# Two graph layers on one core: a changed order of evictions, GpSimd sums, row additions and norm steps within pairs of attention slots

## The chip, the cores and the metric

The kernel runs on one core of one Trainium2 chip. The metric is the device time of one execution in microseconds; a lower time is better. In texts and traces the engines are PE (TensorE, matmul), PEld (its weight loads), DVE (VectorE), ACT (ScalarE), POOL (GpSimd) and SP (SyncE, which issues most DMAs).

## What is computed

The input is `x` (8 graphs, 2048 nodes, 256 features) and one adjacency matrix (2048 x 2048). Two layers follow each other, each with a residual and a layer norm around it:

```python
# layer 0: attention, softmax inside chunks of 256 nodes, summed over the 8 chunks
scores = clip(einsum('bhnd,bhjcd->bhnjc', q, kc) / sqrt(64), -10, 10)
scores = where(mask == 0, -10.0, scores)
attn = softmax(scores, axis=-1)
ctx = einsum('bhnjc,bhjcd->bhnd', attn, vc)
out = ctx @ Wo.T + bo + x
out = layernorm(out) * gamma + beta          # norm "a"
x = layernorm(x + out)                       # norm "b"
# layer 1: graph attention
e = leaky_relu(s_src[:, :, None, :] + s_dst[:, None, :, :], 0.2)
alpha = softmax(where(mask, e, -inf), axis=2)
h_out = elu(einsum('bijh,bjhd->bihd', alpha, Wh))
x = layernorm(x + h_out)                     # norm "c"
```

## The kernel before, in words

All instructions are placed by hand: every engine works through its own list in the order in which the code emits it, and a tile framework adds the semaphores. So the order of the Python statements is the order on each engine.

**Batches and pairs.** The kernel runs over 8 batches (graphs). Layer 0 of a batch is 64 slots: four quarters `q` of 512 query nodes, two head pairs `hp`, eight chunks `c`. Two slots `s0`, `s1` make a pair, so a batch has 32 pairs `p`; within a quarter the pair has the step number `i`, 0 to 7. In batch `b`, layer 1 of batch `b - 1` runs along (`lower`, `along`): four tiles per pair, each made on VectorE by `make` (`e`, L779, three buffers) and multiplied on TensorE by `use` (`pa`, L801). `make` runs two tiles ahead of `use`, so the last pair of a batch finds only two tiles still to make. Batch 0 has no layer 1 beside it, and spends its first pairs on the mask steps (`Masks.step`) instead. Batch 7 leaves the last 18 slots (nine pairs) without it, since these tiles are kept for the stretch that follows. After the last batch, layer 1 of batch 7 runs alone.

**One pair.** In the iteration of pair `p`, `burst(p + 1)` computes the scores of the next pair: four blocks `ps` (L392), each in a pair of PSUM banks. The pairs of banks rotate among three tags (`two_banks`), and the blocks of a pair's two products (`product`, `pc`, L438) take part in that rotation, in the order ps, ps, ps, ps, pc, pc. An output block `po` (L585) or value block `pw` (L627), where a step has one, takes a turn too. VectorE evicts a score block with clip and mask (`evict`, `pr`, L404, from PSUM and one SBUF row tile), ScalarE takes the exponential (`exps`, L427). `product(s)` multiplies with the values on TensorE, and ScalarE copies the result (`raw`, L445). `normalize(s)` takes the reciprocal on VectorE (`rd`, L455) and then does two two-input rows on GpSimd: `part` (L462) and the addition to `acc` (L464).

The statements of the loop stand in this order before: normalize of the last slot; four score blocks with evictions 0 and 1; exp 0 and 1; make; eviction 2, exp 2; use, make, use, make; product s0; eviction 3, exp 3; normalize s0; use, make, use; the late hooks; product s1.

**Between the layers.** When a quarter's context is complete it goes out to DRAM and comes back transposed (`send_context`, `load_context`, `turn_context`). `Between` then does the rest of layer 0 in the pairs of the next quarter, and part of it in the quarter after that: bias, output projection, `y` (L596), norm "a" (`sums`, `squares`, `factors`, `apply`), the factor gamma (`scale`), the residual (`again`, L605), norm "b", the store of `x1D` (`finish`, L610), its transposed load and `turn`, and the value blocks of layer 1 (`values`). Tables (`FIRST_PAIRS`, `ON_ACT`, `LATE_ON`, `LAST_ON_PE`, `NEXT_...`) say at which step `i` and at which of several places in the pair each of these is emitted. The additions of the rows `bo`, `beta` and gamma (L569, L573, L602) run on GpSimd there, and the norm's mean and factors too. The tile `y` has one buffer. `Closing` does the end of layer 1 (residual `h`, norm "c", output) of batch `b - 2` in the first pairs of batch `b`, with its addition on GpSimd.

**Between batches.** After pair 31 a hand-written list `order` mixes the projections of the next batch (`project`: load, turn, keys, values, queries) with the last quarter's `Between` (`steps`, with row additions and statistics on VectorE) and the rest of the one before it (`early`).

Of the kernel before, what the change touches and what calls it, by code (L numbers as in the profile page):

```python
# [8 lines left out]
F32 = mybir.dt.float32  # L9
# [5 lines left out]
ALU = mybir.AluOpType  # L15
# [7 lines left out]
def adj_resnorm_kernel(  # L23
# [37 lines left out]
    assert D == 64 and KC == HP and 2 * D == P and sum(BANKS) == NT  # L61

    SQ = 32
    QS = HP * NK
# [17 lines left out]
    big = ctx.enter_context(tc.tile_pool(name="big", bufs=1))  # L82
    prp = ctx.enter_context(tc.tile_pool(name="prp", bufs=7))
    ep = ctx.enter_context(tc.tile_pool(name="ep", bufs=3))
# [409 lines left out]
    class Norm:  # L494
# [22 lines left out]

        def sums(self, ks):
            for k in ks:
                junk = small.tile([P, F], BF16, tag="junk", name="junk", bufs=1)  # L520
                nc.scalar.activation(
                    junk, self.src[:, k, :], AF.Copy, accum_out=self.mv[:, k, 0:1]
                )

        def centre(self):
            self.mean = small.tile([P, QT], F32, tag="mean", name="mean_" + self.name)
            nc.gpsimd.tensor_scalar(self.mean, self.mv[:, :, 0], -1.0 / F, None, ALU.mult)

        def squares(self, ks):
            for k in ks:  # L530
                junk = small.tile([P, F], BF16, tag="junk", name="junk", bufs=1)
                nc.scalar.activation(
                    junk,
                    self.src[:, k, :],
                    AF.Square,
                    bias=self.mean[:, k : k + 1],
                    accum_out=self.mv[:, k, 1:2],
                )

        def factors(self):  # L540
            self.rs = small.tile([P, QT], F32, tag="rs", name="rs_" + self.name)
            self.off = small.tile([P, QT], F32, tag="off", name="off_" + self.name)
            nc.gpsimd.tensor_scalar(self.rs, self.mv[:, :, 1], 1.0 / F, EPS, ALU.mult, ALU.add)
            nc.gpsimd.tensor_tensor(self.rs, self.rs, nhalf, ALU.pow)
            nc.gpsimd.tensor_mul(self.off, self.mean, self.rs)

# [11 lines left out]
    class Between:  # L558
# [3 lines left out]
        def __init__(self, b, g, sd, waug):  # L562
            self.b, self.g, self.sd, self.waug = b, g, sd, waug
            self.r = load_x(b, g, "xg")
            self.y = blocks.tile([P, QT, F], F32, tag="y", name="y", bufs=1)

        def bias(self, by):
            row = bo_sb.unsqueeze(1).to_broadcast([P, QT, F])
            by.tensor_add(self.r, self.r, row)  # L569

        def shift(self, by):
            row = beta_sb.unsqueeze(1).to_broadcast([P, QT, F])
            by.tensor_add(self.r, self.r, row)  # L573

# [24 lines left out]

        def scale(self, by):  # L600
            row = gamma_sb.unsqueeze(1).to_broadcast([P, QT, F])
            by.tensor_mul(self.y, self.y, row)  # L602

# [39 lines left out]

    FIRST_PAIRS = {
        2: lambda o: o.add((0, 1)),
        3: lambda o: o.add((2, 3)),
    }
    ON_ACT = {
        2: lambda o: o.a.sums((0, 1)),
        3: lambda o: o.a.sums((2, 3)),  # L650
        4: lambda o: o.a.squares((0, 1, 2, 3)),
        5: lambda o: o.a.apply(o.y),
        7: lambda o: o.b2.sums((0, 1, 2, 3)),
    }
    LATE_ON = {
        1: lambda o: o.bias(nc.gpsimd),
        3: lambda o: (o.a.centre(), o.shift(nc.gpsimd)),
        4: lambda o: o.a.factors(),
        5: lambda o: o.scale(nc.gpsimd),
        6: lambda o: o.again(),  # L660
        7: lambda o: o.b2.centre(),
    }
    LAST_ON_PE = {
        1: lambda o: o.output((0, 1)),
        2: lambda o: o.output((2, 3)),
    }
    NEXT_FIRST = {2: lambda o: o.load()}
    NEXT_ON_ACT = {
        0: lambda o: o.b2.squares((0, 1, 2, 3)),
        1: lambda o: o.finish(),  # L670
    }
    NEXT_LATE = {
        0: lambda o: o.b2.factors(),
        3: lambda o: o.turn(),
    }
    NEXT_LAST = {
        4: lambda o: o.values((0, 1)),
        5: lambda o: o.values((2, 3)),
    }
# [176 lines left out]
    class Close:  # L856
# [8 lines left out]

        def add(self, by=nc.vector):
            by.tensor_add(self.h, self.h, self.x)
            self.n = Norm(self.h, "c")
# [43 lines left out]
    HOME = (blocks, "xb", 2)  # L912
    HOME_Y = (blocks, "y", 1)
    HOME_PR = (prp, "pr", 7)

    class Closing:
# [5 lines left out]
        def do(self, s, *kinds):  # L922
            for g, step, *more in self.table.get(s, ()):
                if step not in kinds:
                    continue
                if step == "load":
                    self.of[g] = Close(self.b, g, *more)
                elif step == "finish":
                    self.of[g].finish()
                elif step == "add":  # L930
                    self.of[g].add(*more)
                elif step == "stats":
                    self.of[g].n.stats((0, 1, 2, 3))
                elif step == "most":
                    self.of[g].add_most()
                elif step == "sums":
                    self.of[g].n.sums((0, 1, 2, 3))
                elif step == "centre":
                    self.of[g].n.centre()
                elif step == "squares":  # L940
                    self.of[g].n.squares((0, 1, 2, 3))
                elif step == "factors":
                    self.of[g].n.factors()
# [27 lines left out]

    def closing_of(first, loads):
        table = {}
        for g, (i, (at, home)) in enumerate(zip(first, loads)):
            table.setdefault(at, []).append((g, "load", home))
            table.setdefault(i, []).append((g, "add", nc.gpsimd))
            table.setdefault(i + 1, []).extend([(g, "sums"), (g, "centre")])
            table.setdefault(i + 2, []).extend([(g, "squares"), (g, "factors")])
            table.setdefault(i + 3, []).append((g, "finish"))
        return table  # L980

    CLOSING = closing_of((0, 1, 3, 5), ((-1, HOME), (0, HOME), (2, HOME_Y), (4, HOME)))
    CLOSING_ALONE = {
# [25 lines left out]
    for b in range(B):  # L1009
# [16 lines left out]
        for p in range(PAIRS):  # L1026
# [22 lines left out]
            if p == PAIRS - 2 and b + 1 < B:  # L1049
                turns = [project(b + 1, g) for g in range(NCH)]  # L1050
                turns[0].pop(0)()

            if p:
                normalize(s0 - 1)
            hook(FIRST_PAIRS, NEXT_FIRST)
            if more:
# [4 lines left out]
                exps(*us[1])  # L1061
            hook(ON_ACT, NEXT_ON_ACT)
            if closing:
                closing.do(p, "sums", "squares", "finish")

            if along:
                along.rest(1)
                along.make()
            if more:
                evict(*waiting[1][0], waiting[1][1])  # L1070
                exps(*us[2])
            if along:
                along.use()
                along.make()
                along.use()
                along.make()
            elif not lower and masks.left():
                masks.step()
            product(s0)
            if more:  # L1080
                evict(*waiting[2][0], waiting[2][1])
                exps(*us[3])
            normalize(s0)
            if along:
                along.rest(1)
                along.use()
                along.make()
                along.use()
            elif not lower and masks.left():
                masks.step()  # L1090
            if i == 0 and q:
                send_context(b, q - 1, 1)
            if i == QP // 2:
                send_context(b, q, 0)
            if i == 1 and q:
                turn_context(q - 1, 1)
            if i == QP // 2 + 2:
                turn_context(q, 0)
            hook(LATE_ON, NEXT_LATE)
            if closing:  # L1100
                closing.do(p, "add", "centre", "factors")
            if p == PAIRS - 1 and b + 1 < B:
                turns[0].pop(0)()
            product(s1)
            hook(LAST_ON_PE, NEXT_LAST)
        normalize(SLOTS - 1)
# [4 lines left out]
        group = None  # L1111
        every = tuple(range(QT))

# [9 lines left out]
        def start_next():  # L1123
# [3 lines left out]
        early = [  # L1127
            lambda: before.b2.squares(every),
            lambda: before.b2.factors(),
            lambda: before.finish(),  # L1130
# [6 lines left out]
        steps = [  # L1137
            lambda: group.bias(nc.vector),
            lambda: group.output(every, parts),
            lambda: group.add(every),  # L1140
            lambda: (group.shift(nc.vector), group.a.stats(every)),
            lambda: group.a.apply(group.y),
            lambda: (group.scale(nc.vector), group.again(), group.b2.stats(every)),
            lambda: group.finish(),
# [86 lines left out]
```

## Time and profile before

| What | Value |
|---|---|
| Median of 3 runs | 3864.47 us (3863.78 to 3865.68) |
| The profiled execution's own time | 3871.02 us |
| Its span, first to last instruction | 3869.2 us |
| Mean granted clock of TensorE | 0.985 |
| Loop of batch 0 (pairs 0 to 30) | 291.9 us |
| Loop of batch 1 | 379.0 us |
| Loops of batches 2 to 6 | 382.6 to 384.2 us |
| Loop of batch 7 | 360.6 us |
| From the last pair of a batch to the first scores of the next | 73.0 (batch 0), 79 to 85 us |
| From the last pair of batch 7 to the end | 291.3 us |

The page gives busy time by engine and groups of instructions by line: busy time, mean length of one, then the idle time of the engine ahead of them and who ended it. A line of waits reads: who waited, for whom, microseconds in total, number of times, the longest. A line of a stretch gives its bounds, its length, busy time and instructions of each engine, and then the granted clock, the DMA share and the DMA rate. A loop in the table is measured from the first score matmul of one pair to that of another.

### The profile page before, as it was taken

What the parts mean: (1) busy time and instruction counts of PE and PEld (TensorE: products, weight loads), DVE (VectorE), ACT (ScalarE), POOL (GpSimd) and SP (SyncE); (2) the same over time, 40 slices, a digit from 0 to 9 for tenths busy, and PEclk for the clock granted to TensorE, in tenths of its full rate; (3) what the DMA queues carried; (4) which work ended last, traced back from release to release, by engine and by line L of the source; (5) the groups of instructions that cost most, each with busy time, mean ns of one, the idle gap of its engine ahead of it and who ended that gap; (6) DMA issues with size and microseconds to landing.
All of it is one profiled execution on the core that took longest, in us unless ns stands there. A gap on an engine that the chain in (4) does not pass through costs nothing.

```text
span 3869.2 us, 168899 instructions
## 1 busy us (share of the span) xinstructions
PE 3608.6 (93%) x76884; PEld 2625.2 (68%) x76884; DVE 3037.3 (78%) x3397; ACT 2262.8 (58%) x4211; POOL 1868.2 (48%) x1442
## 2 busy tenths in 40 slices
PE   8999999999999899999999999999999999999787
PEld 5655676766767667676767767777676766776676
DVE  5875688867888488885988848887688866886799
ACT  4776456656656565664756557655566656666322
POOL 0555245545555365553655536555355545555300
PEclk9999999999999999999999999999999999999899
DMA  6743333334333343333433334333443334333354
GB/s 163 159 103 71 87 96 100 105 72 120 100 99 100 72 125 98 104 99 80 118 100 97 93 100 122 97 92 82 106 114 105 103 69 115 102 101 87 85 149 136
DMA packets 635262, 399.03 MB, mean 103 GB/s; under 512 B 423216, under 2 KB 521904, under 8 KB 634544
## 3 DMA queue, kind: packets, MB, share of 16 engines
q1 hardware_dynamic: 584544, 354.53, 36.0%
q10 hardware_dynamic: 50000, 33.70, 2.8%
q8 instruction: 601, 9.85, 1.1%
q14 instruction: 117, 0.96, 0.1%
HBM read 331.22 MB, written 56.89 MB: 100 GB/s over the span
## 4 chain that ended last, share of the span: by engine, by line
PE 53%; DVE 25%; issue 9%; POOL 4%; ACT 4%; DMA 3%; SPq 0%; DVEq 0%; ACTq 0%; POOLq 0%
PE pc L438 15%; PE ps L392 14%; PE pa L801 13%; DVE e L779 10%; DVE pr L404 9%; PE pp L337 4%; PE pw L627 3%; PE pv L353 2%; POOL part L462 2%; POOL xg L569 1%; DMA x1D<-y 1%; PE po L585 1%; ACT y L549 1%; ACT raw L445 1%; DVE y L605 1%
## 5 line engine op out<-in xcount | busy, mean ns | idle before, releaser
L427 ACT ACTIVATE pr<-pr 128x1024 f32<-128x1024 f32 x1024 | 1077.1, 1056 | 960.2 <-DVE pr L404 940.8
L779 DVE SCALAR_TENSOR_TENSOR e<-srow,gd,et 128x1024 f32<-128x1024 f32 x1024 | 1385.0, 1379 | 17.4 <-PE pa L801 13.7
L404 DVE SCALAR_TENSOR_TENSOR pr<-ps,slab 128x1024 f32<-128x1024 f32 x1024 | 1217.5, 1214 | 118.8 <-PE ps L392 90.8
L801 PEld LDWEIGHTS pa<-waug,e 128*64 128x64 f32 x32768 | 1026.4, 140 | 278.9 <-issue 168.3
L801 PE MATMUL pa<-waug,e 128*64 128x65 f32 x32768 | 1100.6, 225 | 80.8 <-DVE e L779 74.9
L462 POOL TENSOR_TENSOR part<-raw,rd 128x512 f32<-128x512 f32 x448 | 634.5, 1416 | 992.5 <-DVE rd L455 982.1
L438 PE MATMUL pc<-vaug,pr 128*64 128x65 f32 x32768 | 1048.4, 223 | 6.4 <-issue 6.0
L392 PE MATMUL ps<-qT,kT 64*64 64x512 f32 x8192 | 977.0, 601 | 74.3 <-DVE pr L404 34.6
L438 PEld LDWEIGHTS pc<-vaug,pr 128*64 128x64 f32 x32768 | 1003.3, 138 | 29.2 <-DVE pr L404 18.1
L464 POOL TENSOR_TENSOR acc<-acc,part 128x512 f32<-128x512 f32 x448 | 668.8, 1493 | 35.1
L392 PEld LDWEIGHTS ps<-qT,kT 64*64 64x64 f32 x8192 | 271.7, 132 | 605.2 <-issue 242.2
L445 ACT COPY raw<-pc 128x520 f32<-128x520 f32 x512 | 297.5, 582 | 66.1 <-PE pc L438 63.0
L455 DVE RECIPROCAL rd<-raw 128x8 f32<-128x8 f32 x512 | 100.7, 197 | 284.7 <-ACT raw L445 284.7
L462 POOL TENSOR_TENSOR acc<-raw,rd 128x512 f32<-128x512 f32 x64 | 117.3, 1833 | 386.3 <-DVE rd L455 386.3
L337 PE MATMUL pp<-xT,wk_sb 128*128 128x512 f32 x256 | 135.7, 680 | 35.3 <-DVE xT L299 31.6
L596 DVE TENSOR_TENSOR y<-po,xg 128x512 f32<-128x512 f32 (+1 forms) x56 | 43.0, 768 | 155.1 <-POOL xg L569 67.7
L833 ACT ACTIVATE sums<-sums,dn 128x64 f32<-128x64 f32 x504 | 131.9, 335 | 21.7 <-DVE dn L827 12.8
L585 PE MATMUL po<-wo_sb,qT 128*64 128x256 f32 (+1 forms) x912 | 124.9, 382 | 12.5 <-DVE qT L482 11.8
L627 PE MATMUL pw<-w_sb,x1T 128*64 128x264 f32 (+1 forms) x800 | 125.8, 392 | 4.0 <-DVE x1T L299 4.0
L337 PEld LDWEIGHTS pp<-xT,wk_sb 128*128 128x128 f32 x256 | 53.7, 218 | 103.8 <-issue 63.5
L353 PE MATMUL pv<-wv_sb,xT 128*128 128x256 f32 x512 | 115.9, 379 | 0.0
L337 PE MATMUL pp<-xT,wq_sb 128*128 128x512 f32 x256 | 115.9, 595 | 0.0
(129 smaller groups left out, 2198.9 us busy)
## 6 DMA issues: line engine op xcount, KB each, us to landing
et<-edgeD SPq DMA_DIRECT2D x512, 256.0 KB, 3.1
slab<-clipD SPq DMA_DIRECT2D x256, 256.0 KB, 3.5
srow<-rowD SPq DMA_DIRECT2D x64, 512.0 KB, 4.9
xg<-in_x_dram SPq DMA_DIRECT2D x32, 512.0 KB, 5.0
x1D<-y ACTq DMA_DIRECT2D x32, 512.0 KB, 4.4
x1g<-x1D SPq DMA_DIRECT2D x32, 512.0 KB, 5.1
out_dram<-x1g SPq DMA_DIRECT2D x30, 512.0 KB, 4.0
ctxD<-acc ACTq DMA_DIRECT2D x56, 256.0 KB, 4.0
```

Of the source, the lines that this page charges most:

```text
L337: nc.tensor.matmul(pps[c], lhsT=w[:, kc, c * P : (c + 1) * P], rhs=st["xT"][:, kc, :], start=(kc == 0), stop=(kc == KC - 1),)
L353: nc.tensor.matmul(pv[:, u, :], lhsT=st["xT"][:, kc, u * P : (u + 1) * P], rhs=wv_sb[:, kc, :], start=(kc == 0), stop=(kc == KC - 1),)
L392: nc.tensor.matmul(ps[z * D : (z + 1) * D, k, :], lhsT=kT[rows, hp, t * P + z * D : t * P + (z + 1) * D], rhs=qT[rows, hp, cols], start=Tr ...
L404: nc.vector.scalar_tensor_tensor(pr, ps, -CLIP, row.unsqueeze(1).to_broadcast([P, 2, CH]), op0=ALU.max, op1=ALU.min,)
L427: nc.scalar.activation(pr, pr, AF.Exp, scale=0.125)
L438: nc.tensor.matmul(pc[z * D : (z + 1) * D, k, to], lhsT=probs[s][u][:, k, i * P + z * D : i * P + (z + 1) * D], rhs=vaug[:, KT * c + u, 2 ...
L445: nc.scalar.copy(raws[s].rearrange("p k i d -> p k (i d)"), pc[:, :, : QT * D1])
L462: nc.gpsimd.tensor_mul(part, raw[:, :, :, :D], rd.to_broadcast([P, 2, QT, D]))
L464: nc.gpsimd.tensor_add(accv, accv, part)
L627: nc.tensor.matmul(pw[z, k, : F + 2 * H], lhsT=self.x1T[:, c, u * P + z.start : u * P + z.stop], rhs=w1_sb[:, c, :], start=(c == 0), stop= ...
L779: nc.vector.scalar_tensor_tensor(e[:, :w], self.rows[n][:, :w], self.gd[:, h, j : j + 1], self.edge[k // JG][:, j % JG, :w], op0=ALU.max, ...
L801: nc.tensor.matmul(self.pa[i // QT][z * D : (z + 1) * D, i % QT, :], lhsT=e[:, i * P + z * D : i * P + (z + 1) * D], rhs=self.waug[:, j, h ...
```

## The change

The order within a pair becomes: normalize of the last slot; four score blocks with evictions 0 and 1; exp 0 and 1; make, use, make; the middle hooks (row additions, turns); product s0; normalize s0; evictions 2 and 3; the hooks on ScalarE; exp 2; use, make, use, make, use; the end hook; product s1; exp 3. The number of tiles made and used per pair stays four. The additions of the rows and the closing addition move from GpSimd to VectorE. `y` gets two buffers and `pr` six instead of seven. Most norm steps move a pair later, `bias` stays at step 1 but goes to the middle of the pair, `again` moves from step 6 to the end of step 7. `sums` folds the factor of the mean into its scale, so `centre` goes, and `factors` does its two scalar rows on VectorE. In `closing`, the last two loads go to the `y` buffers, and the table is written out. After the loop, the statistics of `before.b2` are taken on VectorE (`stats`).

```diff
-    prp = ctx.enter_context(tc.tile_pool(name="prp", bufs=7))
+    prp = ctx.enter_context(tc.tile_pool(name="prp", bufs=6))
...
         def factors(self):
...
-            nc.gpsimd.tensor_scalar(self.rs, self.mv[:, :, 1], 1.0 / F, EPS, ALU.mult, ALU.add)
+            nc.vector.tensor_scalar(self.rs, self.mv[:, :, 1], EPS, None, ALU.add)
+            nc.vector.tensor_scalar(self.off, self.mv[:, :, 0], ROOT_F, None, ALU.mult)
             nc.gpsimd.tensor_tensor(self.rs, self.rs, nhalf, ALU.pow)
-            nc.gpsimd.tensor_mul(self.off, self.mean, self.rs)
+            nc.gpsimd.tensor_mul(self.off, self.off, self.rs)
...
-            self.y = blocks.tile([P, QT, F], F32, tag="y", name="y", bufs=1)
+            self.y = blocks.tile([P, QT, F], F32, tag="y", name="y")
...
-    FIRST_PAIRS = {
-        2: lambda o: o.add((0, 1)),
-        3: lambda o: o.add((2, 3)),
+    FIRST_OF = {
+        3: lambda o: o.add((0, 1)),
+        4: lambda o: o.add((2, 3)),
+    }
+    MIDDLE_OF = {
+        1: lambda o: o.bias(),
+        4: lambda o: o.shift(),
+        7: lambda o: o.scale(),
     }
     ON_ACT = {
-        2: lambda o: o.a.sums((0, 1)),
-        3: lambda o: o.a.sums((2, 3)),
-        4: lambda o: o.a.squares((0, 1, 2, 3)),
-        5: lambda o: o.a.apply(o.y),
-        7: lambda o: o.b2.sums((0, 1, 2, 3)),
+        3: lambda o: o.a.sums((0, 1)),
+        4: lambda o: o.a.sums((2, 3)),
+        5: lambda o: (o.a.squares(every), o.a.factors()),
+        6: lambda o: o.a.apply(o.y),
     }
-    LATE_ON = {
-        1: lambda o: o.bias(nc.gpsimd),
-        3: lambda o: (o.a.centre(), o.shift(nc.gpsimd)),
-        4: lambda o: o.a.factors(),
-        5: lambda o: o.scale(nc.gpsimd),
-        6: lambda o: o.again(),
-        7: lambda o: o.b2.centre(),
+    END_OF = {
+        7: lambda o: o.again(),
     }
-    LAST_ON_PE = {
-        1: lambda o: o.output((0, 1)),
-        2: lambda o: o.output((2, 3)),
+    LAST_OF = {
+        2: lambda o: o.output((0, 1)),
+        3: lambda o: o.output((2, 3)),
     }
-    NEXT_FIRST = {2: lambda o: o.load()}
+    NEXT_FIRST = {3: lambda o: o.load()}
+    NEXT_MIDDLE = {4: lambda o: o.turn()}
     NEXT_ON_ACT = {
-        0: lambda o: o.b2.squares((0, 1, 2, 3)),
-        1: lambda o: o.finish(),
+        0: lambda o: o.b2.sums(every),
+        1: lambda o: (o.b2.squares(every), o.b2.factors()),
+        2: lambda o: o.finish(),
     }
...
     NEXT_LAST = {
-        4: lambda o: o.values((0, 1)),
-        5: lambda o: o.values((2, 3)),
+        5: lambda o: o.values((0, 1)),
+        6: lambda o: o.values((2, 3)),
     }
...
+    CLOSING = {
+        -1: [(0, "load", HOME), (1, "load", HOME)],
+        0: [(0, "add")],
+        1: [(0, "sums"), (1, "add")],
+        2: [(0, "squares"), (1, "sums"), (2, "load", HOME_Y)],
+        3: [(0, "finish"), (1, "squares")],
+        4: [(1, "finish"), (2, "add"), (3, "load", HOME_Y)],
+        5: [(2, "sums")],
+        6: [(2, "squares"), (3, "add")],
+        7: [(2, "finish")],
+        8: [(3, "sums")],
+        9: [(3, "squares")],
+        10: [(3, "finish")],
+    }
```

The loop after the change, from the bursts to the end of a pair:

```python
hook(FIRST_OF, NEXT_FIRST)
if p:
    normalize(s0 - 1)
if more:
    us = units_of(p + 1)
    waiting = burst(p + 1)
    evict(*waiting[0][0], waiting[0][1])
    exps(*us[0])
    exps(*us[1])
if along:
    along.rest(1)
    along.make()
    along.use()
    along.make()
elif not lower and masks.left():
    masks.step()
hook(MIDDLE_OF, NEXT_MIDDLE)
if closing:
    closing.do(p, "add")
...
product(s0)
normalize(s0)
if more:
    for us_ps in waiting[1:]:
        evict(*us_ps[0], us_ps[1])
hook(ON_ACT, NEXT_ON_ACT)
if closing:
    closing.do(p, "sums", "squares", "finish")
...
if more:
    exps(*us[2])
if along:
    along.rest(1)
    along.use()
    along.make()
    along.use()
    along.make()
    along.use()
elif not lower and masks.left():
    masks.step()
hook(END_OF, {})
...
product(s1)
if more:
    exps(*us[3])
hook(LAST_OF, NEXT_LAST)
```

After the loop: `early` begins with `before.b2.stats(every)` in place of `squares` and `factors`.

## The prediction

> **What bounds the kernel now.** I read the page's busy shares first, then who waited for whom, then the stretches of the loop one pair at a time, then single rows of the timeline.
>
> ```profile
> PE 3608.6 (93%) x76884; PEld 2625.2 (68%) x76884; DVE 3037.3 (78%) x3397; ACT 2262.8 (58%) x4211; POOL 1868.2 (48%) x1442
> ```
>
> TensorE is the bound: it idles 261 us of 3869. The only time to win is what it waits, and the waits name VectorE:
>
> ```profile
> PE pa L801 <- DVE e L779: 74.9, 96, 4.0
> PE ps L392 <- DVE pr L404: 34.6, 65, 4.6
> PE ps L392 <- DVE y L596: 29.4, 23, 1.5
> DVE y L596 <- POOL xg L569: 67.7, 23, 3.5
> DVE y L596 <- DMA x1D<-y: 65.5, 8, 11.1
> ```
>
> VectorE stands at `y` (L596) 67.7 us for GpSimd's bias row and 65.5 us for the store of the single `y` buffer, and TensorE's next scores stand behind it. Stretches of single pairs (first scores to first scores; length, busy PE, PEld, DVE, ACT, POOL):
>
> ```profile
> 2050.61:2065.33 14.72, 13.41 (x307) 9.46 (x305) 10.88 (x12) 6.30 (x10) 7.22 (x6) 1.00 0.43 90
> 2065.33:2076.54 11.21, 11.21 (x291) 8.67 (x289) 10.75 (x11) 6.27 (x11) 4.61 (x4) 1.00 0.24 63
> 330.66:338.14 7.48, 7.48 (x163) 4.94 (x161) 5.71 (x7) 4.96 (x9) 3.02 (x4) 1.00 0.02 8
> 338.14:347.39 9.25, 9.25 (x180) 5.91 (x176) 6.07 (x7) 7.60 (x15) 7.47 (x7) 1.00 0.23 58
> 2257.90:2261.30 3.40, 3.40 (x5) 1.35 (x5) 0.00 (x0) 0.07 (x1) 0.00 (x0) 0.50 0.47 159
> ```
>
> A pair beside layer 1 takes TensorE 11.21 us at best, a pair without it 7.48; an output or value block adds 9.25 - 7.48 = 1.77. The first row is such a pair with a block, 14.72 instead of 12.98. The last row shows the clock at a half for 3.4 us after TensorE stood idle for 4.36 us.
>
> [...] an eviction (one input in PSUM) is never stretched, `e` (two SBUF inputs) is.
>
> ```profile
> L404 DVE SCALAR_TENSOR_TENSOR pr<-ps,slab x1024: 1166/1215/1226, 70.8 to 3583.5; 128x1024 f32<-128x1024 f32 x171
> L779 DVE SCALAR_TENSOR_TENSOR e<-srow,gd,et x1024: 1228/1274/3405, 435.4 to 3852.4; 128x1024 f32<-128x1024 f32 x171
> ```
>
> [...] The rows give 2.35 to 2.43 against 1.22 us. [...]
>
> **The chain inside a pair.** Timeline rows (start, length):
>
> ```profile
> 1506.40 1.95 PEld L438 LDWEIGHTS pc<-vaug,pr 128*64 128x64 f32 x64
> 1508.60 0.59 ACT L445 COPY raw<-pc 128x520 f32<-128x520 f32 x1 [0.72 <-PE pc L438]
> 1510.23 0.20 DVE L455 RECIPROCAL rd<-raw 128x8 f32<-128x8 f32 x1
> 1510.34 1.24 DVE L779 SCALAR_TENSOR_TENSOR e<-srow,gd,et 128x1024 f32<-128x1024 f32 x1
> 1510.57 1.91 POOL L462 TENSOR_TENSOR part<-raw,rd 128x512 f32<-128x512 f32 x1 [6.45 <-DVE rd L455]
> 1528.03 1.28 POOL L464 TENSOR_TENSOR acc<-acc,part 128x512 f32<-128x512 f32 x1
> 1528.11 2.28 DVE L779 SCALAR_TENSOR_TENSOR e<-srow,gd,et 128x1024 f32<-128x1024 f32 x1
> ```
>
> So: product start to its copy 2.20, copy 0.6, reciprocal at +2.85, next VectorE row 0.11 later, GpSimd 0.35 after the reciprocal. A GpSimd row that meets an `e` waits for its end (1.91 instead of 1.04), and an `e` that meets a GpSimd row waits too (2.28). From the starts of following rows, evictions come every 1.135, `e` every 1.195; an eviction frees its bank 1.27 after its start.
>
> **The change, part by part.** Put 0 at the first score matmul of a pair.
>
> *Pairs beside layer 1.* New PE order: scores to 3.59, one use to 4.53, product s0 to 6.39, three uses to 9.19, product s1 to 11.21: the same work. New VectorE order: evictions 0 and 1 from 1.16 to 3.5, two `e` to 6.1 (0.2 for GpSimd included), then a row addition; the reciprocal of s0 can come at 4.53 + 2.85 = 7.38. So 1.3 us are free there, and a row addition of 1.17 costs nothing. Then evictions 2 and 3 from 7.49, beside GpSimd's two sums, which end 0.35 + 1.13 + 1.28 = 2.76 after the reciprocal, so the next `e` loses 0.2; two `e` to 12.37, the reciprocal of s1, and eviction 0 of the next pair at 12.48. It must free its bank before the three other score blocks end: 12.48 + 1.27 = 13.75 against 11.21 + 2.69 = 13.90. **The slack is 0.15 us.** What exceeds 1.3 in the first half or 0.15 in the second delays TensorE:
> - `again` now stands after the last `e` of step 7: 1.0, twice a batch (the third falls into the last pair).
> - step 4 of quarters 2 and 3: tail 0.28 + shift 1.17 + turn 1.20, less 1.3 and 0.15: 1.05 with the GpSimd stretch absorbed, twice.
> - squares (2.5 us on ScalarE) now before the third exp and layer 1's tail (1.27): the copy of s1 comes 0.7 late, 0.27 lost, five times. `factors` on VectorE, 0.3, hides where `e` would have waited for GpSimd.
> - closing in batches 2 to 7: pair 2 squares and sums (1.1), pair 3 finish, then squares, with `factors` behind them on VectorE (2.0), pair 6 addition beside tail and turn (1.1), pair 9 0.3: 4.5.
>
> Sum: 10.0 a batch. Before: a batch's 31 stretches should be 7.2 + 30 x 11.21 + 10 x 1.77 = 361.2; batches 2 to 6 took 383.3, so 22.1 were lost, mostly at steps 1 and 2 where `y` waited for the bias. Both go: the bias is on VectorE a step before. Gain 5 x 12.1 = 60; batch 1 (no closing) 17.8 less 5.5 = 12; batch 7's first 23 pairs 10. **Together -83.**
>
> *Pairs without layer 1* (batch 0 and the last nine of batch 7). The three PSUM pairs rotate, so product s1 takes the bank that eviction 2 frees. That eviction used to stand before product s0; now it stands behind its reciprocal, with no uses to cover it: 3.59 + 2.85 + 0.11 + 1.27 = 7.82 instead of 5.46. The pair becomes 9.69 instead of 7.48; with mask steps (17 pairs, 8.43 before) 10.15. Summed over batch 0, against its measured 292 and crediting the waits for the bias that go: +34. The end of batch 7: +10. TensorE now idles 1.9 to 2.2 us in each of these some 40 pairs. Gaps of 1.5 to 2.0 in batch 0 left the clock alone, one of 2.41 halved it. If a pair in two lost 1.7 us it would be 32 us, if none nothing; I take **16**. Together **+60**.
>
> *Between batches.* `y` has two buffers, so L596 starts with its matmul, not 2.5 us later. In the last pair no `e` is left in the second half (the tiles are exhausted), `scale` and `again` are on VectorE, and the next batch's first projection comes 0.6 earlier; GpSimd's last sums end sooner, and v0 starts 1.7 earlier. The chain then runs through ScalarE's key copies before `apply`: 2.4 earlier at k2. Six batches: **-15**. Could be -36, if the half clock at k2 goes too, or +10, if the load of `xg`, which waits for the later `again`, comes late.
>
> *At nothing:* one `pr` buffer fewer, since evictions 2 and 3 now follow the product that frees it; the folded scales of `sums` and `squares`; `centre` gone (0.23 on GpSimd); closing loads moved on SP, whose edge loads run six tiles ahead; VectorE's 117 us of row additions, in the 1.3 us hole except where listed. DMAs keep their number. The store of `x1D` on ScalarE's queue, the load of `x1t` on SP's and its turn move one pair later together; that load waits for a landing of 4.4 us, and the edge loads behind it are six tiles (1.5 pairs) ahead. The send of `ctxD` comes sooner on ScalarE's queue, ahead of exp 2; the sums that it waits for end near 3.9, before ScalarE gets there. The layer-1 end has no edited step.
>
> Sum: -83 + 60 - 15 = **-38 us**. The profiled execution took 3871.0 (span 3869.2), 0.17% over the median of 3864.5; the difference is taken from the median: **3826**.
>
> **The rivals.**
> 1. *The chain closes late* (slower). The slack of 0.15 is worked out from rows of another order. If `e` behind two sums starts later, or GpSimd beside evictions is slower, each of 208 pairs beside layer 1 loses the excess. From 0.15 + 38/208 = 0.33 us it outweighs everything; at 0.45 the time is 3826 + 62 = 3888. For it: nothing in the trace shows two sums, two evictions and two `e` in a row. Against: evictions never stretched.
> 2. *The change gives back what it takes.* The clock halves at every second short pair (+16) and the load of `xg` is late (+25): 3867.
> 3. *All covers hold*: no half clock in the short pairs, -36 between: 3789.
> 4. *It isn't what it says*: the sums still meet `e`. Then the same chain as rival 1, below its point.
>
> **How the numbers follow.** About 0.2% (8 us) is what a measurement here can tell from no change. Forecast (3806 to 3848) 0.42; rival 3 0.12; rival 2 and what lies between 0.22, of it 0.10 faster and 0.12 the same; rival 1, with 4, 0.24. So faster 0.64, same 0.12, slower 0.24. Range 3787 to 3892, from rival 3 to rival 1. The forecast's own is 3806 to 3848.
>
> **What would show it.** Right: pairs beside layer 1 at 11.21 with few exceptions, `e` near 1.28 throughout, no wait of `y` for POOL or for the store; batch 0 longer by some 35 us with PE `pc` waiting for DVE `pr`; PEclk at a half in places there. Wrong: pairs of 11.4 or more everywhere, with PE `ps` waiting for `pr`; or batch 0 unchanged.

## The result, and the profile after

| What | Before | After |
|---|---|---|
| Median | 3865.07 us (3863.78 to 3865.89) | **3800.70 us** (3793.95 to 3802.55) |
| The profiled execution's own time | 3871.02 us | 3793.95 us |
| Loop of batch 0 | 291.9 us | 335.9 us |
| Loops of batches 1 to 6, sum | 2295.7 us | 2202.4 us |
| Loop of batch 7 | 360.6 us | 358.1 us |
| Between batches, after batch 0; after 1 to 6, mean | 73.0; 82.0 us | 75.8; 77.8 us |
| From the last pair of batch 7 to the end | 291.3 us | 290.0 us |

The ratio is 0.9831, 95% interval 0.9814 to 0.9848: 1.7% faster. The profiled execution of after is the fastest of its runs, and that of before lies above all of its timed ones, so the two profiles differ by 77 us where the medians differ by 64. The stretches below are sums of the profiled 77.

The page's first lines of after, busy time by engine and the shares of the chain of waits:

```profile
PE 3570.4 (94%) x76884; PEld 2632.2 (69%) x76884; DVE 3079.9 (81%) x3701; ACT 2237.4 (59%) x4083; POOL 1390.2 (37%) x1202
...
PE 78%; DVE 13%; issue 5%; ACT 3%; DMA 1%; POOL 0%; DVEq 0%; ACTq 0%; SPq 0%; POOLq 0%
```

TensorE idles 222 us instead of 261. In the chain, VectorE had 25% before and GpSimd 4%; now it is 13% and nothing. Who waited for whom (total us, times, longest):

```profile
PE pc L440 <- DVE pr L406: 79.8, 57, 2.1
...
DVE y L602 <- PE po L591: 72.4, 55, 4.4
...
PE pa L805 <- DVE e L783: 38.5, 28, 4.0
...
PE ps L394 <- DVE pr L406: 22.8, 32, 4.3
```

Both waits of `y` that the prediction named (67.7 us for GpSimd's bias, 65.5 us for the store) are gone; `y` waits for its own matmul only. `pa` waiting for `e` has halved from 74.9. The first line is new, and it is the price: product s1 waits for eviction 2. The groups of `e` and of GpSimd's two sums (busy us, mean ns):

```profile
L783 DVE SCALAR_TENSOR_TENSOR e<-srow,gd,et 128x1024 f32<-128x1024 f32 x1024 | 1304.1, 1311 | 20.5 <-PE pa L805 11.2
...
L464 POOL TENSOR_TENSOR part<-raw,rd 128x512 f32<-128x512 f32 x448 | 481.0, 1074 | 1408.0 <-DVE rd L457 1401.4
...
L466 POOL TENSOR_TENSOR acc<-acc,part 128x512 f32<-128x512 f32 x448 | 581.0, 1297 | 35.2
```

Before, these means of `e`, `part` and `acc` were 1379, 1416 and 1493 ns. Of 448 `part` rows, 193 took over 1.2 us before and 16 do now. Stretches of single pairs: a pair beside layer 1; the one after an `again`; one with an output block; a short pair of batch 0; one with a mask step; the 3.41 us before a half-clock period, and most of that period (length, then busy PE, PEld, DVE, ACT, POOL, clock, DMA share, GB/s):

```profile
1547.18:1558.39 11.21, 11.21 (x292) 8.67 (x289) 11.12 (x12) 5.86 (x8) 4.66 (x4) 1.00 0.26 75
1558.39:1570.59 12.20, 11.44 (x293) 8.58 (x289) 11.42 (x14) 8.07 (x18) 3.37 (x3) 1.00 0.45 131
1487.56:1500.56 13.00, 13.00 (x309) 9.56 (x305) 12.46 (x14) 9.25 (x13) 6.03 (x6) 1.00 0.41 112
286.04:295.81 9.77, 7.69 (x162) 5.01 (x161) 7.87 (x9) 4.68 (x8) 3.37 (x3) 1.00 0.09 29
229.36:239.52 10.16, 8.47 (x175) 5.58 (x171) 8.39 (x12) 6.60 (x9) 4.66 (x4) 1.00 0.60 125
254.40:257.81 3.41, 1.36 (x48) 1.22 (x42) 2.66 (x5) 2.58 (x7) 0.98 (x1) 1.00 0.62 98
257.90:261.30 3.40, 3.40 (x64) 3.40 (x64) 1.43 (x3) 1.87 (x5) 2.50 (x3) 0.51 0.27 69
```

The timeline of the first of these pairs, from the end of product s0, shows the new order at work (start, length):

```profile
1554.52 0.20 DVE L457 RECIPROCAL rd<-raw 128x8 f32<-128x8 f32 x1
...
1554.64 2.31 DVE L406 SCALAR_TENSOR_TENSOR pr<-ps,slab 128x1024 f32<-128x1024 f32 x2
1554.87 1.04 POOL L464 TENSOR_TENSOR part<-raw,rd 128x512 f32<-128x512 f32 x1 [3.85 <-DVE rd L457]
...
1555.99 1.29 POOL L466 TENSOR_TENSOR acc<-acc,part 128x512 f32<-128x512 f32 x1
...
1556.86 2.69 DVE L783 SCALAR_TENSOR_TENSOR e<-srow,gd,et 128x1024 f32<-128x1024 f32 x2
...
1559.48 1.21 DVE L611 TENSOR_TENSOR y<-y,xg 128x1024 f32<-128x1024 f32 x1
...
1560.62 0.19 DVE L457 RECIPROCAL rd<-raw 128x8 f32<-128x8 f32 x1
...
1560.73 2.30 DVE L406 SCALAR_TENSOR_TENSOR pr<-ps,slab 128x1024 f32<-128x1024 f32 x2
```

The two sums run beside two evictions without loss (1.04 and 1.29 us, the evictions 2.31) and end 2.76 us after the reciprocal, as predicted; the two `e` lose 0.26 (2.69 instead of 2.43, which the two from 1563.54 on take). `again` (L611) sits ahead of the second reciprocal, and the next pair takes 12.20 instead of 11.21. A short pair of batch 0 in the same view:

```profile
289.63 2.09 PE L440 MATMUL pc<-vaug,pr 128*64 128x65 f32 x64
291.82 0.59 ACT L447 COPY raw<-pc 128x520 f32<-128x520 f32 x1 [1.18 <-PE pc L440]
...
292.44 0.20 DVE L457 RECIPROCAL rd<-raw 128x8 f32<-128x8 f32 x1 [0.61 <-ACT raw L447]
292.56 2.31 DVE L406 SCALAR_TENSOR_TENSOR pr<-ps,slab 128x1024 f32<-128x1024 f32 x2
293.80 2.09 PE L440 MATMUL pc<-vaug,pr 128*64 128x65 f32 x64 [2.08 <-DVE pr L406]
```

Product s0, its copy, the reciprocal, eviction 2 and product s1 follow each other in one string, with TensorE idle for 2.08 us in it.

### The profile page after: what moved, and what is told of

It reads as the page before. It is cut to its first block, busy times and chain, and to the rows that moved or that the text cites. A ratio compares the mean times of both kernels' runs of the same rounds, so it can differ in the third digit from the quotient of the medians.

```text
span 3792.1 us, 168780 instructions
## 1 busy us (share of the span) xinstructions
PE 3570.4 (94%) x76884; PEld 2632.2 (69%) x76884; DVE 3079.9 (81%) x3701; ACT 2237.4 (59%) x4083; POOL 1390.2 (37%) x1202
## 4 chain that ended last, share of the span: by engine, by line
PE 78%; DVE 13%; issue 5%; ACT 3%; DMA 1%; POOL 0%; DVEq 0%; ACTq 0%; SPq 0%; POOLq 0%
PE pc L440 23%; PE ps L394 21%; PE pa L805 19%; PE pp L339 6%; DVE pr L406 4%; DVE e L783 4%; PE pw L633 3%; PE po L591 3%; PE pv L355 2%; ACT raw L447 1%; ACT junk L536 1%; DVE y L611 1%; DMA slab<-clipD 0%; DVE xg L579 0%; ACT y L555 0%
## 5 line engine op out<-in xcount | busy, mean ns | idle before, releaser
L783 DVE SCALAR_TENSOR_TENSOR e<-srow,gd,et 128x1024 f32<-128x1024 f32 x1024 | 1304.1, 1311 | 20.5 <-PE pa L805 11.2
L406 DVE SCALAR_TENSOR_TENSOR pr<-ps,slab 128x1024 f32<-128x1024 f32 x1024 | 1187.9, 1202 | 98.5 <-PE ps L394 90.7
L805 PEld LDWEIGHTS pa<-waug,e 128*64 128x64 f32 x32768 | 1016.1, 139 | 234.0 <-issue 171.2
L440 PE MATMUL pc<-vaug,pr 128*64 128x65 f32 x32768 | 1060.2, 223 | 81.9 <-DVE pr L406 79.8
L805 PE MATMUL pa<-waug,e 128*64 128x65 f32 x32768 | 1081.2, 224 | 44.3 <-DVE e L783 38.5
L464 POOL TENSOR_TENSOR part<-raw,rd 128x512 f32<-128x512 f32 x448 | 481.0, 1074 | 1408.0 <-DVE rd L457 1401.4
L394 PE MATMUL ps<-qT,kT 64*64 64x512 f32 x8192 | 954.7, 599 | 27.3 <-DVE pr L406 22.8
L447 ACT COPY raw<-pc 128x520 f32<-128x520 f32 x512 | 302.8, 591 | 581.0 <-PE pc L440 578.6
L466 POOL TENSOR_TENSOR acc<-acc,part 128x512 f32<-128x512 f32 x448 | 581.0, 1297 | 35.2
L464 POOL TENSOR_TENSOR acc<-raw,rd 128x512 f32<-128x512 f32 x64 | 66.8, 1044 | 379.7 <-DVE rd L457 379.7
L339 PEld LDWEIGHTS pp<-xT,wk_sb 128*128 128x128 f32 x256 | 51.2, 208 | 92.2 <-issue 56.3
L817 ACT COPY sums<-pa 128x260 f32<-128x260 f32 x126 | 41.9, 369 | 115.1 <-PE pa L805 113.6
```

Of the source, the lines that this page charges most:

```text
L339: nc.tensor.matmul(pps[c], lhsT=w[:, kc, c * P : (c + 1) * P], rhs=st["xT"][:, kc, :], start=(kc == 0), stop=(kc == KC - 1),)
L394: nc.tensor.matmul(ps[z * D : (z + 1) * D, k, :], lhsT=kT[rows, hp, t * P + z * D : t * P + (z + 1) * D], rhs=qT[rows, hp, cols], start=Tr ...
L406: nc.vector.scalar_tensor_tensor(pr, ps, -CLIP, row.unsqueeze(1).to_broadcast([P, 2, CH]), op0=ALU.max, op1=ALU.min,)
L440: nc.tensor.matmul(pc[z * D : (z + 1) * D, k, to], lhsT=probs[s][u][:, k, i * P + z * D : i * P + (z + 1) * D], rhs=vaug[:, KT * c + u, 2 ...
L447: nc.scalar.copy(raws[s].rearrange("p k i d -> p k (i d)"), pc[:, :, : QT * D1])
L464: nc.gpsimd.tensor_mul(part, raw[:, :, :, :D], rd.to_broadcast([P, 2, QT, D]))
```

## The experiments

Ratios are to the kernel before, run beside each experiment. "Stalls" is the mean over batches 2 to 6 of what a batch's 31 stretches take above 7.2 + 30 x 11.21 + 1.77 for each block in them. There are ten blocks before; with the norm steps a pair later only nine, since the last value block then falls past the last stretch.

| Kernel | Median, us | Ratio, 95% | Stalls, us | Loop of batch 0, us | `e`, ns |
|---|---|---|---|---|---|
| before | 3865 | 1 | 22.1 | 291.9 | 1379 |
| e10: bias on VectorE | 3823.95 | 0.9904 (0.9885 to 0.9923) | 17.0 | 287.2 | 1383 |
| e2: all rows on VectorE | 3814.32 | 0.9870 (0.9853 to 0.9886) | 16.1 | 292.0 | 1360 |
| e9: e2, norm steps later | 3800.29 | 0.9838 (0.9823 to 0.9853) | 15.4 | 287.4 | 1364 |
| e11: e9 without most sums | 3731.42 | 0.9660 (0.9646 to 0.9675) | 7.4 | 285.5 | 1284 |
| e1: order alone | 3977.05 | 1.0294 (1.0279 to 1.0310) | 31.2 | 347.0 | 1464 |
| e5: e1, turns in the middle | 3889.17 | 1.0065 (1.0050 to 1.0080) | 16.5 | 343.4 | 1463 |
| e6: after, rows on GpSimd | 3866.58 | 1.0008 (0.9999 to 1.0017) | 16.7 | 338.2 | 1451 |
| e4: after, one `y` | 3807.23 | 0.9849 (0.9834 to 0.9864) | 8.3 | 337.8 | 1311 |
| e11b: e4 without most sums | 3792.57 | 0.9817 (0.9803 to 0.9832) | 7.2 | 341.3 | 1281 |
| **after** | 3800.70 | 0.9831 (0.9814 to 0.9848) | 8.3 | 335.9 | 1311 |
| e3: after, eviction 2 earlier in short pairs | 3750.55 | 0.9705 (0.9691 to 0.9720) | 8.3 | 305.5 | 1310 |
| e7: e3's idea with seven `pr` | 3756.59 | 0.9726 (0.9711 to 0.9740) | 8.0 | 300.4 | 1313 |
| e12: before's order in short pairs | 3753.49 | 0.9719 (0.9704 to 0.9733) | 7.9 | 302.8 | 1312 |

**e1_order: the order of the pair alone.** The kernel before with the statements of the pair in the new order, its tables and GpSimd's rows as they were.

> The kernel before with the new order in a pair alone (makes, uses, evictions 2 and 3 behind the sums, hooks on ScalarE behind them); rows on GpSimd, one y, steps of the norm as before. Theory A (the gain beside layer 1 comes from the bias that is ready in time, not from the order): loops of batches 1 to 6 within 4 us of 382, batch 0 at some 335 (+44), the end of batch 7 +9: 3895 to 3925. Theory B (it comes from e that no longer meets GpSimd's sums): loops of batches 1 to 6 some 12 lower, with the same +44 and +9: about 3840.

3977 us: far worse than either theory. TensorE's waits name what neither had listed:

```profile
PEld po L585 <- DVE qT L482: 77.1, 21, 3.9
...
PE po L585 <- DVE qT L482: 67.5, 21, 3.4
```

The turn of the context (L482) was emitted late in the pair, behind the evictions and `e` that had moved there, and the output block at the end of the pair waited for it.

**e5_turns: the turns in the middle.** e1, with this edit:

```diff
+            if i == 1 and q:
+                turn_context(q - 1, 1)
+            if i == QP // 2 + 2:
+                turn_context(q, 0)
             product(s0)
```

> The order alone again (rows on GpSimd, one y, steps as before), but with the turns of the context in the middle of the pair instead of behind its last e. In the first try of the order TensorE's output block waited 3.1 to 3.4 us for that turn in three pairs of every batch, 75 to 80 in all: that goes. Theory A (the order alone gains nothing beside layer 1): 3890 to 3915, loops of batches 2 to 6 at 380 to 386. Theory B (it gains there what e no longer waits): loops near 372, about 3845.

3889 us: the late turn was 88 of e1's 114 us. The time is just under theory A's 3890 to 3915, but the loops of batches 2 to 6 (mean 377.7) lie between A's 380 to 386 and B's 372. What is left of the order alone is a batch 0 of +51.5 and gains of 5.6 per batch beside layer 1. `e` still has a mean of 1463 ns, and GpSimd's three rows take 3.19 to 3.20 us where before has 2.35 to 2.37, a sign that these now meet `e`.

**e2_rows and e10_bias: the rows alone.** The kernel before, with `bias`, `shift`, `scale` and the closing addition on VectorE; and with `bias` alone:

```diff
-        1: lambda o: o.bias(nc.gpsimd),
+        1: lambda o: o.bias(nc.vector),
```

> The kernel before with bias, shift, scale and the closing addition on VectorE alone, at their old places. Theory A: the wait of y for the bias (67.7 us) goes, and with it most of what steps 1 and 2 lost: loops of batches 1 to 6 down by 5 to 8, 3815 to 3830. Theory B: the rows meet GpSimd's sums on VectorE and lengthen its queue: 3855 to 3885.

> The kernel before with one edit: the bias row of the tables (step 1) runs on VectorE and not on GpSimd; the two other rows stay on GpSimd. With all rows and the closing addition on VectorE the kernel before took 3814 us. Theory F, the late bias is nearly all of that gain, since VectorE's wait at y for POOL (67.7 us) goes with it: 3815 to 3830. Theory G, half or more of it comes from GpSimd's other rows, which no longer meet e and the sums: 3835 to 3855, with e at a mean of 1.36 to 1.38 us as before.

3814 and 3824: theory A of the first (its loops down by 5.8 a batch, its time 0.7 us below the range) and theory F of the second held: the bias alone brings 40 of 49 us. In e10 VectorE's wait of `y` for POOL is off the list, and this one stays:

```profile
DVE y L596 <- DMA x1D<-y: 62.8, 9, 9.9
```

The excess of pairs at step 2 goes (1.7 us in three quarters), but that at step 1 (0.9 to 1.7) and those at steps 4 to 7 stay: 17.0 of 22.1 us of stalls were not the late bias.

**e9_later: norm steps a pair later.** e2 with the later tables, before's order in the pair, one `y`, `stats` after the loop.

> The order of before, rows on VectorE, and the steps of the norm a pair later as in the change; one y. Against rows alone (3814) this adds the later steps only. Theory D (the later steps carry the rest of the gain beside layer 1, by taking output block and y apart from the turn): loops of batches 2 to 6 from 377 to some 370, 3765 to 3790. Theory E (the order carries it): 3808 to 3820.

3800 us, between the two theories: a kernel as fast as after that lacks the order in the title.

**e4_one_y and e6_rows_pool: after without one part.** One `y` buffer; and the rows back on GpSimd:

```diff
-            self.y = blocks.tile([P, QT, F], F32, tag="y", name="y")
+            self.y = blocks.tile([P, QT, F], F32, tag="y", name="y", bufs=1)
```
```diff
-            nc.vector.tensor_add(self.r, self.r, row)
+            (nc.vector if self.late else nc.gpsimd).tensor_add(self.r, self.r, row)
```

> The changed kernel with one y buffer (pr stays at six; closing group 3 loads to the other pool). Theory (the second y is what shortens the stretch between batches): each of seven stretches 2.5 to 5 longer, loops unchanged: 3818 to 3835. Rival (the stretch is shorter because GpSimd's last sums end sooner): within 5 us of 3800.

> The changed kernel with the row additions of the loop and the closing addition back on GpSimd, at the changed places. Theory A1 (what counts is that the bias stands more than a pair ahead of y; the engine is second): 3800 to 3815. Theory A2 (a GpSimd row of 2.4 us meets the e and holds the sums up): loops of batches 1 to 6 up by 4 to 8, 3830 to 3860.

3807: the second `y` is worth 6.5 us by medians, though the intervals of the two ratios overlap. The theory (3818 to 3835) and its rival (within 5 of 3800) both missed. It shows between batches, 77.8 instead of 79.5 us. 3867: theory A1 fell, and A2 named the right loss (loops of batches 1 to 6 up by 7.7 each) but put the time too low. Without the rows on VectorE the change is worth nothing; they are worth 66 us in the new order and 49 in the old. The group of `e` in e6 shows why:

```profile
L784 DVE SCALAR_TENSOR_TENSOR e<-srow,gd,et 128x1024 f32<-128x1024 f32 x1024 | 1446.3, 1451 | 17.8 <-PE pa L806 10.8 <-DMA srow<-rowD 3.2
```

TensorE's waits in e6 (after: 79.8 and 22.8):

```profile
PE pc L440 <- DVE pr L406: 91.0, 58, 2.1
...
PE ps L394 <- DVE pr L406: 39.3, 55, 4.4
```

With evictions and sums side by side, GpSimd's rows seem to meet the `e` more: `bo` takes 3.16 us, gamma 2.65 and `beta` 2.39, where before has 2.35 to 2.37, and `e` takes 1451 ns instead of 1311. That the chain of the pair, with a slack put at 0.15 us, passes this on is the author's reading; stalls are 16.7 us against 8.3. `again` also waits for the factor gamma on GpSimd there (15.8 us in eight places); how the 66 us divide was not tried.

**e11_nosum and e11b_nosum: what the sums cost in each order.** e9 and e4, both leaving out the addition of `part` to `acc` for all chunks but the last:

```diff
-        if c:
+        if c == NK - 1:
             nc.gpsimd.tensor_add(accv, accv, part)
```

> Order of before inside the pair, rows on VectorE, norm steps a pair later, one y (a version that took 3800 us), and it leaves out the addition of part to acc for all chunks but the last. Theory B, the sums meet e in this order and that costs time: e falls from a mean of 1364 ns to some 1310, loops of batches 2 to 6 become 3 to 6 us shorter each, 3760 to 3785. Rival, a stretched e is covered here, since TensorE sets the pace: within 5 us of 3800.

> The kernel after with one y buffer (a version that took 3807 us), and it leaves out the same additions of part to acc. Theory B, the sums stand beside evictions here and cost nothing, so leaving them out gains nothing: within 6 us of 3807, e at 1.28 to 1.31 us. Rival, the sums still hold up the chain in this order (they end late for the e behind them): as much gain as in the other order, 3770 to 3790.

Theory B held in its direction, and its ranges missed in both. In the old order leaving out the sums brings 69 us, far more than expected. In the new it brings 12 (by ratios) to 15 (by medians), where the theory had at most 6 and its rival 17 to 37. Stalls fall from 15.4 to 7.4 us in the old order and from 8.3 to 7.2 in the new. The timeline of e9 shows both kinds of meeting:

```profile
1503.16 1.28 POOL L464 TENSOR_TENSOR acc<-acc,part 128x512 f32<-128x512 f32 x1
...
1503.58 1.94 DVE L779 SCALAR_TENSOR_TENSOR e<-srow,gd,et 128x1024 f32<-128x1024 f32 x1
...
1524.14 1.24 DVE L779 SCALAR_TENSOR_TENSOR e<-srow,gd,et 128x1024 f32<-128x1024 f32 x1
...
1524.37 1.91 POOL L462 TENSOR_TENSOR part<-raw,rd 128x512 f32<-128x512 f32 x1 [6.66 <-DVE rd L455]
```

The group of `e` in e9, with all sums:

```profile
L779 DVE SCALAR_TENSOR_TENSOR e<-srow,gd,et 128x1024 f32<-128x1024 f32 x1024 | 1368.6, 1364 | 15.4 <-PE pa L801 11.8 <-DMA srow<-rowD 3.2 <-DVE rd L455 0.2
```

The same group in e11, without most of them:

```profile
L779 DVE SCALAR_TENSOR_TENSOR e<-srow,gd,et 128x1024 f32<-128x1024 f32 x1024 | 1286.8, 1284 | 10.8 <-PE pa L801 7.2 <-DMA srow<-rowD 3.3 <-DVE rd L455 0.2
```

And in e11b, the new order without them (e4, with them: 1311 ns):

```profile
L783 DVE SCALAR_TENSOR_TENSOR e<-srow,gd,et 128x1024 f32<-128x1024 f32 x1024 | 1275.2, 1281 | 20.3 <-PE pa L805 9.3 <-DMA srow<-rowD 3.0
```

An `e` that starts 0.42 us after `acc` takes 1.94 instead of 1.24; a `part` that starts 0.23 after `e` takes 1.91 instead of 1.04. A `part` behind an `e` cost TensorE little: in e11 such meetings remain (176 of 448 `part` over 1.2 us, mean 1434 ns), and the gain is there all the same. What cost time was an `e` behind a running sum: in e9 167 `e` start behind an `acc` (mean 1698 ns) and 37 behind a `part` (1897 ns), in e11 6 and 7. Those that start with no GpSimd row running take 1265 to 1272 ns in e9, e11 and e4.

Beside layer 1 the step from e9 to e4 took the loops of batches 1 to 6 from 2246.9 to 2202.2 us, 44.7 us. Leaving out the sums brings 49.3 there in the old order (2197.6) and 5.8 in the new (2196.4): a difference of 43.5. So nearly all that the order wins there is that sums hold up `e` less. They still meet: in e4 201 `e` start behind an `acc`, but near its end (mean 1434 ns), and 6 behind a `part`. Above the `e` that meet no row, that is some 35 us, against some 96 in e9. From e9 to e4 also go the folded mean, the scalar rows of `factors`, the places of hooks and turns, and one `pr` buffer; that the two kernels without sums stall alike (7.4 and 7.2 us) leaves next to nothing for these beside layer 1.

**e3_fix, e7_seven and e12_best: the short pairs.** In pairs without layer 1, e3 puts eviction 2 behind product s0 and ahead of its reciprocal:

```diff
             product(s0)
+            rest = waiting[1:] if more else []
+            if rest and not along:
+                us_ps = rest.pop(0)
+                evict(*us_ps[0], us_ps[1])
             normalize(s0)
-            if more:
-                for us_ps in waiting[1:]:
-                    evict(*us_ps[0], us_ps[1])
+            for us_ps in rest:
+                evict(*us_ps[0], us_ps[1])
```

e7 puts it ahead of product s0, which takes seven `pr` and, for room, one `y`. e12 gives short pairs before's order of evictions, exps and products; there `x1T` shares the seven buffers of `pr`, so that two `y` fit.

> The changed kernel, with eviction 2 ahead of the reciprocal of s0 in pairs that have no layer 1 beside them. Theory (product s1 waits there for eviction 2 behind copy and reciprocal): the gap of TensorE shrinks by 0.8 us in some 40 pairs, -33, and the half clocks of batch 0 go, up to -20 more: 3745 to 3770. Rival (the pair is bound by something else there, ScalarE or the free pr buffer): 3795 to 3803.

> The changed kernel with one y and seven pr buffers, and eviction 2 ahead of product s0 in pairs without layer 1. Theory: product s1 no longer waits there at all, pairs at 7.5 again: 28 us under the 3750 of the first repair, plus 6.5 for the y: 3715 to 3735. Rival (the rest of the gap is not eviction 2): 3750 to 3760.

> The kernel after, but pairs without layer 1 keep the order of before (evictions 2 and 3 and their exps around product s0, and ahead of its reciprocal); x1T shares the buffers of pr, which are seven then; two y buffers. Theory, nothing but the late evictions made the short pairs long: the loop of batch 0 falls to 287 to 295 us and the time to 3735 to 3748. Rival, with one eviction moved ahead (3750.6 us) the rest is already taken by other waits, or sharing the buffers of pr delays x1T: 3748 or more.

3751, 3757 and 3753 us. e3's theory held; e7 and e12 landed where their rivals said. All three beat both kernels; e3's median is the lowest of those that leave nothing out, though its interval overlaps with those of e7 and e12. What TensorE still waits for at `pc` in e3:

```profile
PE pc L440 <- DVE pr L406: 45.8, 54, 1.3
```

And its waits in e12:

```profile
PE ps L392 <- DVE pr L404: 28.9, 47, 4.2
...
PE ps L392 <- ACT raw L445: 23.8, 31, 2.6
...
PE pc L438 <- DVE pr L404: 13.6, 25, 1.2
```

e3 leaves 0.8 to 1.3 us of the wait in each short pair. In e12 most of that wait is gone, and the next pair's scores wait for ScalarE's copy of product s1 instead (23.8 us where after has 4.4). Its theory, that nothing but the late evictions made short pairs long, fell: batch 0 took 302.8 us, not 287 to 295. The later norm steps alone don't do it: e9, which has them in before's order, took 287.4 us there. Between e9 and e12 lie the places of ScalarE's steps within the pair, the shared buffers and the second `y`, and 10.3 us more of half clock, which by an estimate, half of the time at half clock, cost about 5 us; which of them delays the copy was not tried.

## Why the prediction was right, and where its steps were off

The direction held, and so did the range: the median, 3801, lies within 3787 to 3892, though below the forecast's own 3806 to 3848. The gain was larger than forecast, -64 in medians instead of -38. The two chains that the prediction worked out, of a pair beside layer 1 and of a short pair, came out as drawn. Its reason for the largest term did not.

**The chain of a pair: held.** Most pairs beside layer 1 take 11.21 us. Against the prediction's positions, counted from the first scores at 1547.18: product s0 at +4.58 (4.53), its reciprocal +7.34 (7.38), sums over 2.76 after it (2.76), the two `e` behind them +0.26 (0.2). Rival 1 needed 0.33 us lost in every pair; it fell. Of the signs named, "`e` near 1.28 throughout" did not quite come: the mean is 1.31, with 200 `e` behind the end of `acc` at 1.43.

**Losses that remain beside layer 1: 8.3 a batch, not 10.0.** Term by term:

| Term | Predicted, us | Measured, us |
|---|---|---|
| `again`, twice | 2.0 | 2 x 0.99 |
| Step 4 of quarters 2 and 3 | 2.1 | 2 x 0.50 |
| Squares ahead of the third exp | 5 x 0.27 | 0.5 in pairs 5, 13, 21 and 29 |
| Closing, pairs 2, 3, 6, 9 | 4.5 | 0.91 + 1.85 + 0.57 = 3.3, in pairs 3, 4 and 6 |
| Not listed | 0 | 1.5, of it 0.95 in pairs 7 and 8 |

**Why the stalls of before went: the wrong reason.** The prediction took 22.1 us a batch as lost, "mostly at steps 1 and 2 where `y` waited for the bias". From pair 9 on, these steps hold 9.2 of the 22.1, and e10 shows that the late bias was 5.1 of all. With all rows 6.0 are explained, and with later steps 6.7. The largest piece, 15.4 to 8.3, came from the pair's order (e4 against e9, with e11 and e11b for the cause): `e` stood behind sums, which the prediction had priced only for the new order, at 0.2. By its reason the bias alone should have brought most of the -83; e10 brought 30.7 us in the loops of batches 1 to 6. The term came near because the losses of before were measured against an undisturbed batch, whatever disturbs it, and the losses of after were worked out from the chain. That the change also removed the loss that the prediction hadn't seen was luck.

**-83 beside layer 1: measured -105** (93.3 in batches 1 to 6, 11.3 in the first three quarters of batch 7). 10.6 of it is no gain: with the value blocks a step later, one of 1.77 us falls out of the stretches of each of six batches (and of batch 0). The prediction's sum missed that move. The rest of the difference is the smaller losses.

**+60 in the short pairs: measured +53** (44.0 in batch 0, 8.8 in the last pairs of batch 7). The wait was named and sized right: 9.77 against 9.69 for the plain pair, 10.16 against 10.15 with a mask step, `pc` waiting for `pr` 2.08. The clock was the part off: it stood at a half for 23.9 us of batch 0's loop against 6.8, and for 6.8 us of batch 7's last pairs against none. A product of 64 matmuls that starts in such a stretch (257.83) took 3.64 us, one at full clock (269.16) 2.09. Taken as half of the time at half clock, an estimate, that costs (23.9 - 6.8) / 2 = 8.5 us and 3.4 us, where 16 were put in for all short pairs.

Gaps of 2.08 us within pairs were followed by a half clock six times in batch 0's loop. The starts of these half clocks lie whole multiples of 3.41 us apart; counted on from them, the loop divides into intervals of that length. Of the 13 gaps of 2.08 us the six that lie whole within one such interval, which leaves TensorE 1.33 to 1.36 us of work in that interval, were followed by a half clock. The seven that straddle two intervals were not. Of the gaps of 1.64 to 1.69 us in pairs with a mask step three lie whole within an interval, and none was followed by a half clock. So whether a gap of 2.08 us cost clock depended here on where it fell. In e4, e6 and e11b it is the same: 23 intervals with 1.33 or 1.34 us of work in batch 0's loop, and a half clock after each. In e3, whose gaps are 0.8 to 1.3 us, the half clock in that loop is down to 3.4 us.

**-15 between batches: measured -25** after batches 1 to 6, and -36 with the value blocks that moved there counted off at 1.77. Half clocks in these stretches fell from 37.5 to 20.5 us, which by the same estimate is 8.5 of it. -36 is the end that the prediction kept for rival 3. Along the edits the mean stretch goes from 82.0 to 80.7 us with the rows (e2), to 80.5 with the later steps and a value block more in it (e9), to 79.5 with the order (e4) and to 77.8 with the second `y`. What within each of these does it was not tried.

**What the whole consists of.** Along one path of edits, by medians: rows -49 (e2), later steps -14 (e9), order with the smaller edits beside it +7 (e4), second `y` -6.5. The last two are within the noise of single comparisons, since the intervals overlap. The +7 is 44.7 us won beside layer 1 and 56.3 lost in the loops of batches 0 (+50.4) and 7 (+5.9), and smaller gains between batches. The parts don't simply add: the order with the turns set right (e5) made the kernel before 26 us slower.

## What to carry to other kernels

An instruction order that wins where a long list of other work covers the critical wait can lose where this cover is missing: write the order for each kind of iteration, as e3 does for 50 us, and check who waits in the shortest one. Take the loss of a loop against an undisturbed iteration first, then attribute it step by step; a wait with a name and a total (here `y` for the bias) may be less than half of it. When two rows collide, ask which one starts second and who waits for it: here GpSimd's `part` behind `e` (1.91 us instead of 1.04) was cheap, and `e` behind a sum (1.94 instead of 1.24) delayed TensorE.

## What the runs showed of the hardware that was not expected

The stretch of `e` behind a running sum (1.94 us, started 0.42 after an `acc` of 1.28) fits a wait for that row's end and not a slower pace beside it: 0.42 + 0.70 lost is within 0.2 of 1.28. It ended 1.08 us after the sum. So did, in the traces of before and after, each `e` that started with 0.2 us or more of a `part` or `acc` still to run: 148 and 151 of them, 1.08 to 1.09 us after that row's end. The expected size was off: leaving out 384 of 448 sums was taken to bring 3 to 6 us per batch in the old order, and brought 7.9 (loops of batches 2 to 6, 374.8 to 366.9 us).

A gap of 2.08 us of TensorE was followed by half the clock when it fell whole into one of the intervals of 3.41 us counted from the half clocks' starts, in six of six cases in batch 0's loop after the change, and in none of the seven cases where it straddled two.
